# A recurrent graph layer: far targets scaled on ScalarE one node later, and five of them instead of four at places 1 to 3

## The chip, the cores and the metric

The kernel runs on one core of a Trainium2 chip (trn2). The core has a matrix engine, TensorE (PE in the profile, with its weight loads as PEld), and three engines for elementwise work: VectorE (DVE), ScalarE (ACT) and GpSimd (POOL). SyncE (SP) issues most of the DMAs. The metric is the time of one execution on the device in microseconds (us); lower is better.

## The reference, cut to what matters

The network has four layers over 64 graphs of 256 nodes with 256 features, and `adj` as each graph's weighted adjacency matrix. Layer 0 is a recurrence: node i sees a weighted sum of all other nodes' states, where the nodes before it have already been renewed.

```
d = sum(adj, -1);  dinv = 1/d (0 where d is 0)
norm_adjT = swapaxes(adj, 1, 2) * dinv[:, :, None]
for i in range(256):                       # a scan: one node after the other
    x     = h_e[:, i]
    x_par = einsum('bj,bjd->bd', norm_adjT[:, i], h)
    r, z  = sigmoid(x @ W_ioux.T + b_ioux + x_par @ W_iouh.T + b_iouh)
    hc    = tanh(x @ W_coux.T + b_coux + (x_par * r) @ W_couh.T + b_couh)
    h[:, i] = z * x_par + (1 - z) * hc
x = layernorm(x + h)
```

Layers 1 to 3 are a graph convolution and two attention layers, each with a residual and a layer norm. The change does not touch them.

## The kernel before, in words

**Tiling.** In the recurrence one tile of 128 x 128 holds a whole node: 64 graphs times two halves of the 256 features on the partitions, 128 features along the free side. The loop `for now in range(N)` is unrolled at build time and runs over the 256 nodes n; inside a `manual_schedule` the order of instructions on each engine is the order of the program text. U = 8 nodes make a block, and p = n % 8 is called the node's place here.

**Who adds what to whom.** `ACC` holds, for each node still to come, the weighted sum of the states it depends on; `sums[a]` is the tile of block a. A finished state j has to be added to all its later targets. They are shared out by distance:

- The next target, j + 1, gets it through the chain itself (`xp` from `zcc`, line 866).
- Targets up to the end of the next block are the list `to`, first target n + 1 where j = n - 1. The far end of the list, `FAR[p]` targets, goes to GpSimd; the rest, `near`, goes to VectorE as one *push* each: line 630, a multiplication by the weight and an addition to ACC in one instruction, which reads the state from PSUM (`keep`).
- At places 0 and 1 `behind` gives GpSimd eight more targets of the state that closed a block, in two groups of four.
- Everything older comes out of matrix products: `late` (from a ring `Hw` of states in SBUF, which DMAs fill from `hs`) and `early` (from states that were written to HBM, `Hd`). PE does such pieces as *fills* between the chain's own matmuls, ACT copies them out of PSUM (`copy_later`, line 256), DMAs carry them to and fro, and GpSimd adds them to ACC (lines 818 and 876).

**GpSimd's part.** `push_far` multiplies the state `hs` by the weights of all its far targets into the tile `far` (line 663, one instruction for all) and adds this to ACC (line 667). `far` has one buffer. Ahead of it, in each node, GpSimd makes `ready` (line 805), the next node's sum times dinv.

**The chain of a node.** PE transposes xp, ACT copies it to `xpT` (line 614); `next_of(copies, n)` may put one copy after it. PE makes the gate r (`rc`, `h_part`, line 605), ACT its sigmoid `rs` (line 824), PE transposes it, VectorE multiplies it with xpT (`rT`, line 828). Then VectorE makes `zx` and `v` (lines 846 and 853), PE the candidate, ACT its tanh (line 861), VectorE `zcc` (line 863) and the next xp (line 866). Pushes stand in two places on VectorE: `push(1)` and `push(5)` ahead of rT, and `push(3)` between v and zcc. What is left of a state's pushes comes in the next node. `x_part` (line 597) makes the part of the gates that depends on x alone, for the next node, on PE, after tanh's input.

Of the kernel before, what the change touches and what calls it, by code (L numbers as in the profile page):

```python
# [9 lines left out]
F32 = mybir.dt.float32  # L10
BF16 = mybir.dt.bfloat16
AF = mybir.ActivationFunctionType
# [7 lines left out]
P = 128  # L20
# [50 lines left out]
def _recurrence(tc, ident, Hd, x, adj, W_ioux, b_ioux, W_iouh, b_iouh, W_coux, b_coux, W_couh, b_couh, wide, then):  # L71
# [19 lines left out]
    nc = tc.nc  # L91
# [7 lines left out]
    XB = 4  # L99
    NG = B // 4  # L100
    HB = B // 2
    FAR = (2, 4, 4, 4, 4, 4, 3, 4)

    with ExitStack() as ctx:
        const = ctx.enter_context(tc.tile_pool(name="r_const", bufs=1))
# [42 lines left out]
        tmp = stage.enter_context(tc.tile_pool(name="r_setup", bufs=1))  # L148
# [41 lines left out]
        for w in range(2):  # L190
            first = (w * T - W + T // 2) % W
# [50 lines left out]
        copies = []  # L242
# [3 lines left out]
        def next_of(queue, n):  # L246
            if queue:
                queue.pop(0)(n)
# [344 lines left out]
        def x_part(G, n, kc, gates):  # L593
            a, u = divmod(n, U)
            h, i = divmod(u, U // 2)
            for o in range(2):
                nc.tensor.matmul(  # L597
                    G[o * B:(o + 1) * B], xqT[a, i // 2][:, i % 2, kc, h * B:(h + 1) * B],
                    WxT[:, kc, o, gates], start=False, stop=False, skip_group_check=True,
                )  # L600
# [9 lines left out]
        def flip(src, tag, n):  # L610
            pt = ps.tile([P, P], F32, tag="flip", name=f"{tag}_ps_{n}")
            nc.tensor.transpose(pt, src, ident)
            t = new(tag, n, 1)
            nc.scalar.copy(t, pt)  # L614
            return t

        def new(tag, n, bufs=2):
            return work.tile([P, P], F32, tag=tag, name=f"{tag}_{n}", bufs=bufs)

        def cell(j, m, count=1):  # L620

            a, u = divmod(m, U)
            k, i = divmod(m, T)
            return sums[a][:, u:u + count, :], tables[k]["S"][:, LAG + j - k * T, i:i + count]

        def push(count):
            for _ in range(min(count, len(pushes))):
                m, j = pushes.pop(0)
                acc, s = cell(j, m)
                nc.vector.scalar_tensor_tensor(  # L630
                    acc[:, 0, :], keep[:, j % 2, :], s, acc[:, 0, :], ALU.mult, ALU.add
                )
# [10 lines left out]
        def state(n):  # L643

            h = keep[:, n % 2, :]
            nc.vector.tensor_add(h, zcc, keep[:, 2, :])
            hs = new("hs", n, 7)
            nc.vector.tensor_add(hs, zcc, keep[:, 2, :])
            ring_in.append((n, hs))
            return hs  # L650

        def into_ring():
            n, hs = ring_in.pop(0)
            for o in range(2):
                to = Hw[n % W::W] if n < N - U else Hd[n]
                nc.sync.dma_start(to[..., o * P:(o + 1) * P], hs[o * B:(o + 1) * B])

        def push_far(j, hs, first, count):

            acc, s = cell(j, first, count)  # L660
            tmp = work.tile([P, 4, P], F32, tag="far", name=f"far_{j}_{first}", bufs=1)
            shape = [P, count, P]
            nc.gpsimd.tensor_mul(  # L663
                tmp[:, 0:count, :], hs.unsqueeze(1).to_broadcast(shape),
                s.unsqueeze(2).to_broadcast(shape),
            )
            nc.gpsimd.tensor_add(acc, acc, tmp[:, 0:count, :])  # L667

        tables = {k: {} for k in range(NB)}
        sums = {}  # L670
# [41 lines left out]
        work = ctx.enter_context(tc.tile_pool(name="r_work", bufs=2))  # L712
# [16 lines left out]
                x_part(G, 0, kc, gates)  # L729

        keep = ps.tile([P, 4, P], F32, tag="keep", name="keep")
        xp = new("xp", 0)
        nc.vector.tensor_scalar(xp, sums[0][:, 0, :], dinv[:, 0:1], None, ALU.mult)

        zcc = hs = None
        late_side = background = None
        behind = []
        x_left = x_side()
# [18 lines left out]
        for now in range(N):  # L757
            n = now
            k, i = divmod(n, T)
            p = n % U  # L760
            last = n + 1 == N

            xpT = flip(xp, "xpT", n)
            next_of(copies, n)

            far = []
            if n:

                assert all(j == n - 2 for _, j in pushes)
                hs = state(n - 1)  # L770
                end = min((n - 1) // U * U + 2 * U, N)
                to = list(range(n + 1, end))
                near = to[:len(to) - min(FAR[p], len(to) - 1)] if to else []
                far = to[len(near):]
                pushes += [(m, n - 1) for m in near]
                pushes.sort()
                if p == 0:

                    behind = [(n - 1, hs, m, 4) for m in range(end, min(end + U, N), 4)]

                if p > 3 or n >= N - U:
                    for _ in range(min(2, len(ring_in))):
                        into_ring()
# [23 lines left out]
                    dinv[:, n + 1:n + 2].to_broadcast([P, P]),  # L807
                )
            push(5)
            if far:  # L810
                push_far(n - 1, hs, far[0], len(far))
            if behind:
                push_far(*behind.pop(0))
            if p in (3, 4):
                half = slice((p - 3) * U // 2, (p - 2) * U // 2)
                for first, part in early_parts:
                    acc = sums[first // U][:, half]
# [32 lines left out]
            if not last:  # L850
                Sd = tables[kk]["Sd"][:, ii:ii + 1]
                v = keep[:, 3, :]
                nc.vector.scalar_tensor_tensor(v, zx, Sd, ready, ALU.mult, ALU.add)
                push(3)
                for kc in range(2):
                    x_part(rc, n + 1, kc, slice(0, 2))
                z = ps.tile([P, P], F32, tag="z", name=f"z_ps_{n + 1}")
                nc.scalar.copy(z, bias_z)
                for kc in range(2):
                    x_part(z, n + 1, kc, 2)  # L860
            nc.scalar.activation(c, c, AF.Tanh)
            zcc = new("zcc", n, 1)
            nc.vector.tensor_mul(zcc, zc, c)
            if not last:
                xp = new("xp", n + 1)
                nc.vector.scalar_tensor_tensor(xp, zcc, Sd, v, ALU.mult, ALU.add)
            for _ in range(2):
                next_of(copies, n)
# [554 lines left out]
def kernel(ctx: ExitStack, tc: tile.TileContext, ins, out):  # L1423
# [14 lines left out]
    def load_layers(load):  # L1438
        weights.extend(
            _load_layers(nc, wide, load, ins["L1_gnn_W"], ins["L1_gnn_b"], l2, l3)  # L1440
        )

    _recurrence(
        tc, ident, Hd, x, adj,
        *(ins["L0_gnn_" + n] for n in (
# [44 lines left out]
```

## Time and profile before

| | |
|---|---|
| median of 3 runs | 3351.88 us (3350.82 to 3364.95) |
| the profiled execution, its own time | 3353.51 us |
| its span, first to last instruction | 3351.7 us |
| VectorE busy | 2554.5 us (76%) |
| ScalarE busy | 1838.6 us (55%) |
| GpSimd busy | 1845.0 us (55%) |
| TensorE busy | 3131.6 us (93%) |
| pushes, line 630 | 1712, mean 343 ns |
| far multiplications, line 663 | 313, mean 973 ns |
| far additions, line 667 | 313, mean 1189 ns |

The profile follows one execution instruction by instruction. Busy time is the time in which an engine has at least one instruction of its own at work, and matmuls are pipelined, so that a busy PE need not be at its peak. A row of a group gives the engine, the operation, the tiles (out<-in), how often it stands, its busy time, the mean length of one, and the idle time of the engine just before. The waits view says which instruction waited for which, and for how long in total. In a timeline the square bracket shows how long the engine had been idle before an instruction and what released it.

The loop over the nodes fills the stretch from 139 to 1475 us; layers 1 to 3 come after it.

### The profile page before, as it was taken

Reading aid. Unit: us, or ns where it says so; the run is one execution under the profiler, and the core shown is the slowest. Engines: PE = TensorE matmul, PEld = TensorE weight load, DVE = VectorE, ACT = ScalarE, POOL = GpSimd, SP = SyncE. Lnnn points to the kernel's source line nnn. Section 1 sums busy time; section 2 is a strip of 40 time slices with the busy share of each in tenths; the row PEclk is TensorE's granted clock in tenths of the full one; section 3 lists DMA queues with packets and bytes.
Section 4 is the critical chain, followed back from the end, with each engine's and each line's share of the span. In section 5 each row is a group of like instructions: output and inputs, shape, how many; then the busy total and the mean of one; then the engine's idle time right before and its main releaser. Section 6 shows DMA issues by size and latency. Waiting matters only on the chain.

```text
span 3351.7 us, 78940 instructions
## 1 busy us (share of the span) xinstructions
PE 3131.6 (93%) x28584; PEld 2311.5 (69%) x28584; DVE 2554.5 (76%) x7381; ACT 1838.6 (55%) x4754; POOL 1845.0 (55%) x2165
## 2 busy tenths in 40 slices
PE   5799998998879998969999999999999999999997
PEld 4566665555545555547888888888888888888885
DVE  3487777776667878856888888888888888888885
ACT  0155554544445544535666666666666666666664
POOL 2377777766667878833444444444444444444443
PEclk7899999999999999989999999999999999999999
DMA  9856685788877675241221211122222222222210
GB/s 292 247 161 156 168 194 152 179 198 207 204 181 178 163 174 152 65 105 47 56 57 54 57 56 54 54 55 58 57 58 58 58 57 58 57 58 58 58 33 20
DMA packets 528608, 364.62 MB, mean 109 GB/s; under 512 B 246620, under 2 KB 494568, under 8 KB 522984
## 3 DMA queue, kind: packets, MB, share of 16 engines
q1 hardware_dynamic: 510520, 342.63, 39.6%
q10 hardware_dynamic: 17696, 16.91, 1.5%
q8 instruction: 229, 3.75, 0.5%
q14 instruction: 163, 1.34, 0.1%
HBM read 240.78 MB, written 99.61 MB: 102 GB/s over the span
## 4 chain that ended last, share of the span: by engine, by line
PE 77%; DMA 8%; DVE 7%; issue 2%; SPq 2%; ACT 2%; POOL 1%; DVEq 0%; ACTq 0%; POOLq 0%
PE mm L997 14%; PE rc L605 6%; PE rc L597 4%; PE s L1195 4%; PE mm_2f L997 3%; PE mm_3v L997 3%; PE mm_3f L997 3%; PE mm_2v L997 3%; PE late L521 3%; PE mm_t L997 3%; PE mm_2s L997 3%; PE mm_g L997 3%; PE mm_2w L997 3%; PE o L1230 3%; DVE ACC L630 3%; PE o L1221 3%
## 5 line engine op out<-in xcount | busy, mean ns | idle before, releaser
L1207 POOL TENSOR_TENSOR p3s<-p 128x256 f32<-128x256 f32 x512 | 358.9, 733 | 364.7 <-ACT p L1205 364.6
L630 DVE SCALAR_TENSOR_TENSOR ACC<-keep,S,ACC 128x128 f32<-128x128 f32 x1712 | 479.1, 343 | 16.9 <-POOL ACC L876 11.2
L997 PE MATMUL mm<-xT,weights 128*128 128x256 f32 x2048 | 483.7, 384 | 2.7 <-ACT xT L1094 2.7
L997 PEld LDWEIGHTS mm<-xT,weights 128*128 128x128 f32 x2048 | 386.0, 191 | 79.9 <-issue 25.5
L1204 DVE TENSOR_TENSOR p<-s,neg 128x512 f32<-128x512 f32 x512 | 317.6, 682 | 118.2 <-PE s L1195 118.2
L667 POOL TENSOR_TENSOR ACC<-ACC,far 128x384 f32<-128x384 f32 (+1 forms) x313 | 372.1, 1189 | 24.5
L663 POOL TENSOR_TENSOR far<-hs,S 128x384 f32<-128x384 f32 (+1 forms) x313 | 304.7, 973 | 4.7
L1205 ACT ACTIVATE p<-p 128x512 f32<-128x512 f32 x512 | 292.4, 626 | 1.6 <-DVE p L1204 1.6
L961 ACT ACTIVATE y<-y,shift,rstd 128x256 f32<-128x256 f32 x512 | 272.9, 599 | 26.6 <-DVE shift L959 22.7
L597 PE MATMUL rc<-WxT,xqT 128*64 128x256 f32 x2048 | 274.8, 390 | 1.1 <-issue 1.1
L1119 ACT ACTIVATE qk<-mm,weights 128x256 f32<-128x256 f32 x256 | 107.5, 471 | 301.9 <-PE mm L997 301.9
L805 POOL TENSOR_TENSOR ready<-ACC,dinv 128x128 f32<-128x128 f32 x255 | 102.1, 400 | 304.7 <-DVE ACC L630 304.2
L1108 POOL TENSOR_TENSOR y<-y,g 128x512 f32<-128x512 f32 x64 | 81.0, 1266 | 301.8 <-issue 301.8
L1244 DVE RECIPROCAL rT<-o 128x256 f32<-128x256 f32 x128 | 223.7, 1748 | 0.3 <-PE o L1221 0.2
L949 DVE BATCH_NORM_STATS2 st<-y 128x6 f32<-128x256 f32 x512 | 209.6, 409 | 13.1 <-POOL y L1108 10.3
L521 PE MATMUL late<-Hw,An 64*32 64x256 f32 x3840 | 166.7, 400 | 42.1 <-DMA Hw<-hs 18.8
L605 PE MATMUL rc<-WhT,rT 128*64 128x128 f32 x2048 | 172.5, 290 | 35.6 <-DVE rT L828 33.2
L824 ACT ACTIVATE rs<-rc 128x128 f32<-128x128 f32 x256 | 71.1, 278 | 245.0 <-PE rc L605 245.0
L605 PEld LDWEIGHTS rc<-WhT,rT 128*64 128x64 f32 x2048 | 109.1, 138 | 133.2 <-DVE rT L828 110.8
L953 POOL TENSOR_TENSOR rstd<-rstd,mhalf 128x2 f32<-128x2 f32 x256 | 173.8, 697 | 47.9 <-DVE rstd L952 34.6
L1066 POOL TENSOR_TENSOR dis<-dis,mhalf 128x2 f32<-128x2 f32 x64 | 44.9, 702 | 273.2 <-DVE dis L1065 261.8
L605 PE MATMUL rc<-WhT,xpT 128*64 128x128 f32 x2048 | 169.4, 286 | 18.1 <-ACT xpT L614 18.1
(162 smaller groups left out, 7255.4 us busy)
## 6 DMA issues: line engine op xcount, KB each, us to landing
xX<-in_x_dram ACTq DMA_DIRECT2D x16, 1024.0 KB
Us<-xu SPq DMA_DIRECT2D x64, 256.0 KB
xq<-in_x_dram SPq DMA_DIRECT2D x64, 256.0 KB
ACC<-Us SPq DMA_DIRECT2D x32, 512.0 KB
Es<-eu SPq DMA_DIRECT2D x64, 256.0 KB
early_sb<-Es SPq DMA_DIRECT2D x32, 512.0 KB
xin<-in_x_dram SPq DMA_DIRECT2D x64, 256.0 KB
ad<-in_adj_dram SPq DMA_DIRECT2D x64, 256.0 KB
```

The lines of the kernel that those rows point to most:

```text
L521: nc.tensor.matmul(pb[g][q * T:(q + 1) * T, e, :], An[rows, b].rearrange("p u s -> p (u s)"), Hw[rows, b, :], start=True, stop=True,)
L597: nc.tensor.matmul(G[o * B:(o + 1) * B], xqT[a, i // 2][:, i % 2, kc, h * B:(h + 1) * B], WxT[:, kc, o, gates], start=False, stop=False, s ...
L605: nc.tensor.matmul(G[o * B:(o + 1) * B], hT[:, kc * B:(kc + 1) * B], WhT[:, kc, o, g], start=False, stop=(kc == 1), skip_group_check=True,)
L630: nc.vector.scalar_tensor_tensor(acc[:, 0, :], keep[:, j % 2, :], s, acc[:, 0, :], ALU.mult, ALU.add)
L663: nc.gpsimd.tensor_mul(tmp[:, 0:count, :], hs.unsqueeze(1).to_broadcast(shape), s.unsqueeze(2).to_broadcast(shape),)
L667: nc.gpsimd.tensor_add(acc, acc, tmp[:, 0:count, :])
L961: nc.scalar.activation(y[:, c, :], y[:, c, :], AF.Identity, bias=shift[:, c:c + 1], scale=rstd[:, c:c + 1],)
L997: nc.tensor.matmul(pm[:, c, :], lhsT[:, k, c * P:(c + 1) * P], rhs[:, k, :], start=(k == 0), stop=(k == 1),)
L1204: nc.vector.tensor_add(p, s_ps[i], self.neg3)
L1205: nc.scalar.activation(p, p, AF.Exp, scale=ISQ)
L1207: nc.gpsimd.tensor_add(both, p[:, 0, :], p[:, 1, :])
L1244: nc.vector.reciprocal(rT, o_ps[:, 1, :])
```

## The change

`push_far` is split. `scale_far` reserves the far tile and lets ACT multiply the state by the weight of the first `begun` far targets, one activation (Copy, with the weight as its scale) for each; it returns a function that lets GpSimd multiply the targets that are left and add all of them to ACC. In the loop, `scale_far` is called right after the copy of xpT, for the far targets of the state that the node before had listed. GpSimd's part then comes at the old spot in this node, one node later than before. `begun` is 4, or 2 where copies are queued, and not more than there are targets. The groups of `behind` are still multiplied and added by GpSimd alone.

FAR rises by one at places 0 to 3, and the tile `far` from four to five targets. `push(3)` between v and zcc becomes `push(2)`. `xp` has one buffer instead of two.

```diff
-    FAR = (2, 4, 4, 4, 4, 4, 3, 4)
+    FAR = (3, 5, 5, 5, 4, 4, 3, 4)
...
         def push_far(j, hs, first, count):
+            scale_far(j, hs, first, count, 0)()
+
+        def scale_far(j, hs, first, count, begun):
             acc, s = cell(j, first, count)
-            tmp = work.tile([P, 4, P], F32, tag="far", name=f"far_{j}_{first}", bufs=1)
-            shape = [P, count, P]
-            nc.gpsimd.tensor_mul(
-                tmp[:, 0:count, :], hs.unsqueeze(1).to_broadcast(shape),
-                s.unsqueeze(2).to_broadcast(shape),
-            )
-            nc.gpsimd.tensor_add(acc, acc, tmp[:, 0:count, :])
+            tmp = work.tile([P, 5, P], F32, tag="far", name=f"far_{j}_{first}", bufs=1)
+            for e in range(begun):
+                nc.scalar.activation(tmp[:, e, :], hs, AF.Copy, scale=s[:, e:e + 1])
+
+            def finish():
+                if begun < count:
+                    shape = [P, count - begun, P]
+                    nc.gpsimd.tensor_mul(
+                        tmp[:, begun:count, :], hs.unsqueeze(1).to_broadcast(shape),
+                        s[:, begun:count].unsqueeze(2).to_broadcast(shape),
+                    )
+                nc.gpsimd.tensor_add(acc, acc, tmp[:, 0:count, :])
+
+            return finish
...
-        xp = new("xp", 0)
+        xp = new("xp", 0, 1)
...
-        zcc = hs = None
+        zcc = hs = far = None
...
             xpT = flip(xp, "xpT", n)
+            begun = 2 if copies else 4
             next_of(copies, n)
+            add_far = far and scale_far(*far, min(begun, far[-1]))
...
-                near = to[:len(to) - min(FAR[p], len(to) - 1)] if to else []
-                far = to[len(near):]
+                near = to[:len(to) - max(0, min(FAR[p], len(to) - 2))]
+                far = (n - 1, hs, to[len(near)], len(to) - len(near)) if near != to else []
...
-            if far:
-                push_far(n - 1, hs, far[0], len(far))
+            if add_far:
+                add_far()
...
-                push(3)
+                push(2)
...
-                xp = new("xp", n + 1)
+                xp = new("xp", n + 1, 1)
```

## The prediction

> **What bounds the kernel now.** I read the busy time of the stretch that layer 0's loop fills, then the waits inside it, then the timeline of single nodes. The windows view gives the loop (columns: busy us of PE, weight loads, DVE, ACT, POOL):
>
> ```profile
> 139.00:1475.00 1336.00, 1215.21 (x15980) 772.74 (x15978) 1014.43 (x3601) 660.55 (x2188) 961.73 (x1054) 0.98 0.66 166
> ```
>
> 256 nodes in 1336 us are 5.22 us a node. No engine is full, so the nodes hang on a chain. The waits view of the same stretch (us in total, times, longest) shows its links, and that GpSimd hardly holds anybody:
>
> ```profile
> ACT rs L824 <- PE rc L605: 245.0, 255, 4.7
> DVE zcc L863 <- ACT rc L861: 123.1, 135, 7.1
> DVE rT L828 <- PE rT_ps L826: 112.7, 175, 4.1
> PE late L521 <- DMA Hw<-hs: 18.8, 7, 5.6
> DVE ACC L630 <- POOL ACC L876: 11.2, 4, 5.0
> DVE keep L853 <- POOL ready L805: 9.9, 2, 6.1
> ```
>
> Each node runs xpT (ACT), rc (PE), rs (ACT), its transpose (PE), rT (DVE), rc again (PE), tanh (ACT, L861), zcc and xp (DVE), the next xpT. The timeline of a node at place 2 (start us, us) shows where pushes matter:
>
> ```profile
> 1132.98 0.27 ACT L614 COPY xpT<-xpT_ps 128x128 f32<-128x128 f32 x1 [0.36 <-PE xpT_ps L612]
> ...
> 1134.23 0.28 ACT L824 ACTIVATE rs<-rc 128x128 f32<-128x128 f32 x1 [0.98 <-PE rc L605]
> ...
> 1134.93 0.29 DVE L828 TENSOR_TENSOR rT<-rT_ps,xpT 128x128 f32<-128x128 f32 x1 [0.16 <-PE rT_ps L826]
> ...
> 1135.92 0.87 DVE L630 SCALAR_TENSOR_TENSOR ACC<-keep,S,ACC 128x128 f32<-128x128 f32 x3
> 1136.18 0.26 ACT L861 ACTIVATE rc<-rc 128x128 f32<-128x128 f32 x1 [0.45 <-PE rc L605]
> ...
> 1136.71 0.28 DVE L863 TENSOR_TENSOR zcc<-zc,rc 128x128 f32<-128x128 f32 x1
> ...
> 1137.79 0.27 ACT L614 COPY xpT<-xpT_ps 128x128 f32<-128x128 f32 x1 [0.36 <-PE xpT_ps L612]
> ```
>
> The reader is to see two things. Three pushes sit behind rT, and zcc starts straight after them (no idle time is shown), 0.53 us after tanh, where it starts 0.29 us after tanh at the places without them: VectorE is late there. And ACT is idle for 0.98 us just before rs, waiting for PE. The change spends that idle time.
>
> **What the Trainium skill says.** "ScalarE: Activation LUTs", section "What ACT_TABLE_LOAD costs": an ACTIVATE with immediate operands takes 186 ns + 0.833 ns an element, each pointer operand adds about 93 ns, and neighbours overlap by about 93 ns. The trace agrees: the layer norm's ACTIVATE (256 elements, two pointers) would be 186+213+186 = 585 ns, the trace has 598 as median, and four of them take
>
> ```profile
> 2005.86 2.08 ACT L961 ACTIVATE y<-y,shift,rstd 128x256 f32<-128x256 f32 x4
> ```
>
> so (2.08-0.60)/3 = 0.493 us from start to start. "Perfetto Trace Analysis", section "Tensor Engine Instruction": ACT, DVE and GpSimd are strict first in, first out. What stands behind a waiting or late scale on ACT therefore waits too; the rows of before do not show it at this spot. "SBUF — State Buffer", section "SBUF: two separate sides": GpSimd holds off a VectorE operation only if that is in a two-port mode or has two SBUF inputs. A push reads one operand from PSUM; its pitch is 0.26 us in nodes with and without GpSimd work. So a lighter GpSimd makes the pushes no faster: priced at nothing.
>
> **The change part by part.**
>
> *Pushes.* FAR goes from 29 to 33 targets in eight nodes. VectorE loses one push behind rT at places 1, 2 and 3, and one ahead of rT at place 0. The latter is worth nothing: VectorE idles 0.37 us ahead of rT there. Behind rT a push is 0.26 us, but tanh to next xpT cannot fall below 1.49 us: that is what places 4 to 7 take, where x_part and the transpose on PE set it. Places 1 and 2 take 1.61 (1136.18 to 1137.79), so 0.12 each is gained; place 3, whose last push depends on the one before it, takes 1.74, so 0.25. Over 30 blocks, the few nodes held elsewhere left out: 3.8 + 4.0 + 7.8, some **15.5 us gained**. PE is late next.
>
> *Scales on ACT.* In the built order 916 activations stand between xpT and rs: four at places 0 and 2 to 6, three at place 7, and at place 1 mostly one copy and two. No row has this operation. From L961: 0.493 less 128 elements (0.107) less one pointer (0.093) is 0.293 us a scale. From below, 0.265 if the pointer is hidden in part; from above, 0.386 if a second operand is fetched like a pointer. I take 0.293. Then rs can start 4 x 0.293 + 0.17 (the step between neighbouring activations such as zc and z) = 1.34 us after xpT; with three 1.05; at place 1 0.16 + 0.61 + 0.29 + 0.17 = 1.23. Today rs starts after 1.09 at place 0, 1.25 at places 1 to 3, and at places 4 to 7 after 1.08 (no fill on PE ahead of it), 1.22 (one fill) or 1.5 to 1.8. What stands queued behind the scales is rs, and behind rs the transpose, rT and the rest of the chain. Per place, over 31 blocks:
> - place 0: 0.25 x 31 = 7.6 us
> - place 1: nothing (1.23 below 1.25); place 7: nothing (1.05 below 1.08)
> - place 2: 0.09 x 29 = 2.7 us, and the wait below
> - place 3: 0.09 x 17 = 1.6 us; in 12 nodes VectorE reaches rT 0.22 later than the transpose and covers it
> - place 5: 1.0 us, place 6: 10 x 0.26 + 14 x 0.12, about 4.0 us
> - place 4: mostly under the push below.
>
> *Waits that are new.* The far buffer has one copy, so the first scale waits for the GpSimd add of the node before. This bites at place 2 only: at place 1 GpSimd starts its far add after the second scale (1.5 us after xpT), then adds three (1.00), scales four (1.04) and adds four (1.28) for the block behind, and with 0.08 between them ends 5.0 us after xpT. The next xpT comes at 4.81 - 0.12 = 4.69. I put the first scale, and so rs, 0.11 later in 24 nodes: 2.6 us. Second, at place 4 the push behind rT goes to the target that GpSimd adds as its fifth in that very node. Its add takes 1.28 + 0.28 = 1.55 us (rows of 2, 3 and 4 targets: 0.726, 1.002, 1.276) and ends about 3.2 to 3.4 us after xpT, while the push stands at 2.8 to 3.1 today. With the scales' own delay place 4 loses 4.4 us. Loss in all: 7.6+5.3+1.6+4.4+1.0+4.0 = **24 us**.
>
> *What covers the loss.* Place 0 lasts 5.44 us undisturbed, but 7.08 on average: in some blocks PE waits at the late fill (L521) for hs rows that DMAs bring to Hw. A delay of places 4 to 0 vanishes in such a wait as far as it reaches: taken block by block up to 7.6 us; I take 6, as some landings shift along. Without that cover it is paid in full.
>
> *Nothing.* The single xp buffer (its last reader is an earlier VectorE operation); the lighter GpSimd, as `ready` is waited for twice only; SP, which gets no DMA more or less. GpSimd loses nearly all far multiplications, at about 1 us each, beside the chain.
>
> Sum: -15.5 + 24 - 6 = +2.5, say **+3 us**. The profiled execution took 3353.51 (span 3351.7), 1.6 above the median of the runs, 3351.88; on the median's footing I predict 3355.
>
> **The rivals.**
> - *A draw* (0.62): as summed. All three prices cancel: between 0.28 and 0.32 us a scale the sum runs from -4 to +14 us.
> - *The scales fit* (faster): if rs is not late, only the push saving is left, -15.5 us, and -22 if PE gives way too (0.24 + 0.24 + 0.26 a block); only the second passes 0.5%. For it: 0.98 us of idle ACT. Against it: four scales at any price above 0.23 need more than 1.09 at place 0. About 3330 to 3336.
> - *ACT becomes the chain* (slower): a scale costs 0.386, where four stand in a row they hold rs until 4 x 0.386 + 0.17 = 1.71 us. Worked through the same list the loss is 92 us, less 15.5 and up to 18 of cover: +58, 3410. It passes 0.5% from about 0.33 us a scale. For it: no row of this form. Against it: L961 fits the page's pointer price.
> - *The change does nothing on ACT*: if the scales kept to GpSimd, only the later adds and pushes would remain; the built order excludes it.
>
> **How the numbers follow.** A measurement of this kernel can tell about 0.5% (17 us) from no change. Same 0.62. Slower 0.25: 0.12 for a scale over 0.33 us, the rest for no cover at place 0 together with more waits on GpSimd. Faster 0.13, for scales below 0.26 with more stalls absorbed. The range 3335 to 3382 takes in scale prices of about 0.26 to 0.335 and the disturbance by DMA waits (the runs shown spread over 14 us); the full second-operand case is left out.
>
> **What would show it.** In the profile after: activations of 128x128 to `far`, mean near 0.39 us and 0.29 from start to start; ACT busy up by some 290 us; GpSimd down by about 160; rs 1.34 us behind xpT at places 0 and 2; the wait of rs for PE nearly gone; tanh to xpT 1.49 at places 1 to 3; pushes 1592 instead of 1712. I am wrong if rs keeps its 1.1 us at place 0, if places 1 to 3 gain more than 0.25, or if a wait of ACT for GpSimd's add totals over 10 us.

## The result, and the profile after

The changed kernel takes 3354.73 us as median of 12 runs (3345.69 to 3363.22), the kernel before 3356.49 us beside it; the ratio is 0.9995 with a 95% interval of 0.9981 to 1.0009. No change can be told, as forecast. The execution in the profile took 3362.24 us, a long one of this kernel, so its total says little; its single nodes say a lot.

The windows view of the loop (columns as before):

```profile
136.00:1478.00 1342.00, 1213.24 (x15955) 773.55 (x15957) 978.13 (x3475) 901.31 (x3100) 805.80 (x915) 0.97 0.66 165
```

ACT rose from 661 to 901 us in the loop, GpSimd fell from 962 to 806, VectorE from 1014 to 978. The waits view of the loop:

```profile
DVE rT L841 <- PE rT_ps L839: 152.1, 205, 4.8
DVE zcc L876 <- ACT rc L874: 124.5, 134, 6.9
POOL ACC L676 <- ACT far L667: 96.3, 139, 2.9
PEld rT_ps L839 <- ACT rs L837: 87.2, 254, 0.6
ACT rs L837 <- PE rc L605: 17.4, 33, 3.1
PE late L521 <- DMA Hw<-hs: 16.3, 7, 3.8
DVE ACC L630 <- POOL ACC L676: 10.0, 31, 0.5
```

The wait of rs for PE, 245.0 us before, has gone to 17.4. That is no gain: rs now comes after the scales instead, PE's transpose waits longer for rs (62.7 to 87.2), and VectorE waits longer for the transpose ahead of rT (112.7 to 152.1). GpSimd's add now waits for ACT's scales (third line); that delays the chain only where VectorE or ACT in turn waits for the add. The last line is such a place: the push at place 4, 31 times, once a block. The timeline of a node at place 2, in the same block as the node shown of before:

```profile
1133.97 1.27 POOL L676 TENSOR_TENSOR ACC<-ACC,far 128x512 f32<-128x512 f32 x1
...
1134.98 0.27 ACT L614 COPY xpT<-xpT_ps 128x128 f32<-128x128 f32 x1 [0.24 <-PE xpT_ps L612]
...
1135.28 1.28 ACT L667 ACTIVATE far<-hs,S 128x128 f32<-128x128 f32 x4
...
1136.46 0.26 ACT L837 ACTIVATE rs<-rc 128x128 f32<-128x128 f32 x1
...
1138.13 0.61 DVE L630 SCALAR_TENSOR_TENSOR ACC<-keep,S,ACC 128x128 f32<-128x128 f32 x2
1138.38 0.26 ACT L874 ACTIVATE rc<-rc 128x128 f32<-128x128 f32 x1 [0.45 <-PE rc L605]
...
1138.68 0.29 DVE L876 TENSOR_TENSOR zcc<-zc,rc 128x128 f32<-128x128 f32 x1
...
1139.87 0.27 ACT L614 COPY xpT<-xpT_ps 128x128 f32<-128x128 f32 x1 [0.24 <-PE xpT_ps L612]
```

Both halves stand in it. Behind rT there are two pushes; zcc starts 0.30 us after tanh (1138.38 to 1138.68) and no longer 0.53, and tanh to the next xpT takes 1.49 us instead of 1.61. Ahead of it, rs starts 1.48 us after xpT instead of 1.25. The first scale starts as soon as GpSimd's add (1133.97 + 1.27 = 1135.24) has ended. The node takes 4.89 us instead of 4.81: what the pushes save here, the later rs takes back and a little more.

By place, medians of the xpT-to-xpT time in us, worked out from the starts of line 614 in the traces (at place 0 the undisturbed time, the lower quarter of the nodes):

| place | 0 | 1 | 2 | 3 | 4 | 5 | 6 | 7 |
|---|---|---|---|---|---|---|---|---|
| before | 5.44 | 4.81 | 4.81 | 5.02 | 4.76 | 5.22 | 4.63 | 4.63 |
| after | 5.67 | 4.69 | 4.90 | 4.79 | 4.80 | 5.22 | 4.73 | 4.63 |

### The profile page after: what moved, and what is told of

Its sections match the earlier page's. It is cut to its first block, busy times and chain, and to the rows that moved or that the text cites. A ratio compares the mean times of both kernels' runs of the same rounds, so it can differ in the third digit from the quotient of the medians.

```text
span 3360.5 us, 79856 instructions
## 1 busy us (share of the span) xinstructions
PE 3134.5 (93%) x28584; PEld 2315.3 (69%) x28584; DVE 2520.3 (75%) x7261; ACT 2080.4 (62%) x5670; POOL 1689.1 (50%) x2028
## 4 chain that ended last, share of the span: by engine, by line
PE 75%; DMA 7%; ACT 6%; DVE 4%; POOL 3%; issue 3%; SPq 2%; ACTq 0%; POOLq 0%; DVEq 0%
PE mm L1010 14%; PE rc L605 5%; PE rc L597 5%; PE s L1208 4%; PE mm_2f L1010 4%; PE mm_3v L1010 4%; PE mm_t L1010 3%; ACT far L667 3%; PE mm_3f L1010 3%; PE mm_2v L1010 3%; PE mm_g L1010 3%; PE mm_2s L1010 3%; PE mm_2w L1010 3%; PE o L1243 3%; PE tr_x L1000 3%
## 5 line engine op out<-in xcount | busy, mean ns | idle before, releaser
L676 POOL TENSOR_TENSOR ACC<-ACC,far 128x640 f32<-128x640 f32 (+2 forms) x312 | 404.6, 1297 | 143.8 <-ACT far L667 96.3
L630 DVE SCALAR_TENSOR_TENSOR ACC<-keep,S,ACC 128x128 f32<-128x128 f32 x1592 | 447.6, 343 | 24.3 <-POOL ACC L676 10.0
L667 ACT ACTIVATE far<-hs,S 128x128 f32<-128x128 f32 x916 | 295.3, 394 | 1.2
L962 DVE BATCH_NORM_STATS2 st<-y 128x6 f32<-128x256 f32 x512 | 209.6, 409 | 13.5 <-POOL y L1121 10.7
L521 PE MATMUL late<-Hw,An 64*32 64x256 f32 x3840 | 169.5, 407 | 39.5 <-DMA Hw<-hs 16.3
L841 DVE TENSOR_TENSOR rT<-rT_ps,xpT 128x128 f32<-128x128 f32 x256 | 74.2, 290 | 155.0 <-PE rT_ps L839 154.8
```

The source lines that it names most:

```text
L630: nc.vector.scalar_tensor_tensor(acc[:, 0, :], keep[:, j % 2, :], s, acc[:, 0, :], ALU.mult, ALU.add)
L667: nc.scalar.activation(tmp[:, e, :], hs, AF.Copy, scale=s[:, e:e + 1])
L962: nc.vector.bn_stats(st, y[:, c, :])
```

## The experiments

**One half each.** The first run keeps the saving of the pushes and gives all scales back to GpSimd, in the state's own node:

```diff
             next_of(copies, n)
-            add_far = far and scale_far(*far, min(begun, far[-1]))
...
-            if add_far:
-                add_far()
+            if far:
+                push_far(*far)
```

> The push half of the change alone: FAR, five targets and push(2) as in the changed kernel, but GpSimd scales every far target itself and in the state's own node, as before. Theory (two effects that cancel): the saving of the pushes behind rT stands alone, rs keeps 1.09 us behind xpT at place 0 and 1.25 at places 1 to 3, tanh to the next xpT is about 1.49 us at places 1 to 3, and the time is 10 to 16 us below before. Rival A (waits for DMAs set the pace, so neither half moves the time): within 4 us of before. Rival B (the relief of GpSimd is what pays for the scales): GpSimd is now fuller than before, so slower than before by 10 us or more.

Measured: 3347.07 us beside 3354.59 of before, ratio 0.9974 (0.9962 to 0.9987): 7.5 us faster by the medians, 9 by the ratio. Places 1 to 3 take 4.69, 4.69 and 4.72 us, rs keeps 1.09 and 1.25. Rival A and rival B are out: the half moves the time, and with a GpSimd that is fuller than before. The gain is smaller than the 10 to 16 us expected. In this trace places 1 to 3 took 13.5 us less over 30 blocks and place 0 took 9.7 more; but it is one trace of each kernel, and the runs of one kernel differ by 4 to 6 us (standard deviation). The first place to look is the late fills (L521), where PE waits for the DMAs that carry states to the ring. The number before the first arrow of such a row is PE's idle time ahead of the fills, in us. Before:

```profile
L521 PE MATMUL late<-Hw,An 64*32 64x256 f32 x3840 | 166.7, 400 | 42.1 <-DMA Hw<-hs 18.8 <-DMA Hs<-Hd 5.5 <-POOL ACC L667 5.2
```

and in this run:

```profile
L521 PE MATMUL late<-Hw,An 64*32 64x256 f32 x3840 | 169.1, 407 | 42.3 <-DMA Hw<-hs 22.5 <-DMA Hs<-Hd 7.2 <-DMA Es<-eu 5.8
```

More of it is put down to the ring's DMAs (18.8 to 22.5), but the whole is the same, 42.1 and 42.3. So these rows don't show where the rest of the saving went.

The second run has the scales, but FAR and the third push as before:

```diff
-    FAR = (3, 5, 5, 5, 4, 4, 3, 4)
+    FAR = (2, 4, 4, 4, 4, 4, 3, 4)
...
-                push(2)
+                push(3)
```

> The scale half alone: ACT scales up to four far targets one node later, but FAR and push(3) as before. Theory: rs 1.34 us behind xpT at places 0, 2, 3, 4 and 6, tanh to xpT stays 1.61 to 1.74 at places 1 to 3; by place 7.6 + 2.7 + 1.6 + 2.3 + 1.0 + 4.0 = 19 us lost, some 6 of it covered by DMA waits at place 0: 11 to 19 us above before. Rival A: within 4 us of before. Rival B: GpSimd loses its multiplications, so faster by 5 us or more.

Measured: 3362.90 us, ratio 1.0023 (1.0013 to 1.0034): 8 us slower. rs starts 1.34 us behind xpT at places 0, 2, 3, 4 and 6, as worked out. Rivals A and B are out; the loss is on the right side, but below the lower end of 11 us. The two halves, -0.26% and +0.23%, make up the change's -0.05%.

**How many scales.** The changed kernel with three scales at most:

```diff
-            begun = 2 if copies else 4
+            begun = 2 if copies else 3
```

> The changed kernel with at most three scales on ACT in a node instead of four; GpSimd multiplies one target more. Theory: three scales let rs start 1.05 us behind xpT, ahead of PE everywhere, so rs is no later than before at places 0, 3, 6 (1.09, 1.25, 1.08 to 1.22); left are the saving of the pushes, 15.5 us, and at place 4 the push that waits for GpSimd's add, 4 to 6 us: 8 to 13 us below before. Rival A: within 4 us of before. Rival B (the loss comes from the wait of ACT for GpSimd's add and from the delay by one node, not from how many scales there are): as the changed kernel.

Measured: 3355.03 us, ratio 0.9999 (0.9988 to 1.0011): a miss. By its total both rivals would do, for it is within 4 us of before and like the changed kernel; the trace and the next run speak against them. rs is on time (1.09 at place 0, 1.25 at places 1 to 3), and places 1 to 3 take 4.69 us each, so that part held. Place 4 did not: 5.01 us instead of 4.76, some 9 us over 30 blocks. The timeline of a place 4 in this run:

```profile
243.39 1.55 POOL L676 TENSOR_TENSOR ACC<-ACC,far 128x640 f32<-128x640 f32 x1
...
244.57 0.26 ACT L874 ACTIVATE rc<-rc 128x128 f32<-128x128 f32 x1 [0.31 <-PE rc L605]
...
244.97 0.35 DVE L630 SCALAR_TENSOR_TENSOR ACC<-keep,S,ACC 128x128 f32<-128x128 f32 x1 [0.55 <-POOL ACC L676]
245.24 0.28 DVE L876 TENSOR_TENSOR zcc<-zc,rc 128x128 f32<-128x128 f32 x1
```

The push, and zcc behind it on the same engine, wait 0.55 us for the far add, and zcc comes 0.67 us after tanh. The fourth scale's work had moved to GpSimd, ahead of this add. Another 9 us or so sit at places 5 to 7, in single long nodes of this one trace; place 0 did not grow in it. The fourth run takes both waits for GpSimd away:

```diff
-    FAR = (3, 5, 5, 5, 4, 4, 3, 4)
+    FAR = (3, 5, 5, 5, 5, 4, 3, 4)
...
-            begun = 2 if copies else 4
+            begun = 0 if p == 1 else 3
```

> As the run with three scales, and the two waits for GpSimd taken away: no scale on ACT at place 1, so that GpSimd ends its groups there before the next xpT, and FAR 5 at place 4 too, so that no push behind rT goes to a target that GpSimd adds to in the same node. Theory: nothing but the saving of the pushes is left: 12 to 17 us below before, rs as before at all places, no wait of a push for the far add. Rival A: within 4 us of before. Rival B: no better than the run with three scales, since those two waits cost nothing.

Measured: 3351.55 us, ratio 0.9985 (0.9975 to 0.9995): 3 us faster by the medians, 5 by the ratio; place 4 back at 4.75 us, places 1 to 3 at 4.69 to 4.76, rs on time everywhere. It beats the run with three scales by some 4 us (4.2 by the means of the runs, with a 95% uncertainty of 3, as in all that follows), so rival B falls, but it stays far from 12 to 17, and so near 4 that its total alone doesn't exclude rival A. Again place 0 grew, by 6.6 us over 30 blocks.

**The ring's DMAs left out.** Those runs left one question: is the price of a push too high, or does place 0 swallow the saving? In each of these kernels the DMAs into the ring can be left out. The late products then work on zeros, so their share of the result is missing, while their instructions stay:

```diff
             n, hs = ring_in.pop(0)
-            for o in range(2):
+            for o in range(2 if n >= N - U else 0):
```

> The kernel before without the DMAs that carry each state from hs into the ring Hw (only the last eight, which go to HBM, stay). The late products then work on zeros: their share of the result is left out, their instructions stay. It is the reference for the two runs beside it. Theory (place 0 waits in part of the blocks for these DMAs): place 0 falls from a mean of 7.1 us to below 6, 25 to 40 us below before. Rival (place 0 is long by other DMA traffic): less than 10 us below before.

> The push half alone, with the same DMAs left out (the late products work on zeros). Theory (a saving at places 1 to 3 is given back where place 0 then waits longer for the ring's DMAs): without these waits the saving of the pushes shows in nearly every block, 12 to 16 us below the run without the ring of the kernel before. Rival (the price of a push behind rT was simply set twice too high): 6 to 10 us below it, as with the ring.

> The changed kernel with the same DMAs left out (the late products work on zeros). Theory: no cover is left for the scales and none takes the pushes' saving away, so 24 less 15.5, some 6 to 12 us above the run without the ring of the kernel before. Rival (gain and loss cancel whatever the DMAs do): within 4 us of it.

Measured, in this order: 3279.96, 3271.11 and 3288.79 us (3354.79 for before on that chip; the ratios to before are 0.9777, 0.9749 and 0.9796, each within 0.0021). The first was expected 25 to 40 us below before and is 75 below: place 0 falls to 5.27 us in nearly all blocks, under the 5.44 that I had taken as undisturbed. The row of the late fills in it, 1.1 us of idle time in place of 42.1:

```profile
L521 PE MATMUL late<-Hw,An 64*32 64x256 f32 x3840 | 162.1, 388 | 1.1 <-issue 1.1
```

The changed kernel is 8.8 us above its reference by the medians, near the 8.5 that gain and loss sum to without cover; by the means it is 5.4 above, with an uncertainty of about as much, so the rival (within 4 us) is not excluded. Above the push half beside it the changed kernel stands by 17.7 us (16.3 by the means, uncertainty about 5). The push half is 8.9 below its reference, which is inside the rival's 6 to 10 and not the theory's 12 to 16. With five runs each that is not settled, so both were run again with the fourth kernel beside them:

> The kernel before without the DMAs into the ring, once more, as the reference on this chip. Every theory: 2.0 to 2.4% below before.

> The push half without the DMAs into the ring, once more, since the first comparison fell between two readings. Theory (the saving shows in nearly every block): 11 to 16 us below the run beside it of the kernel before without the ring. Rival (the price was set too high): 6 to 9 us below it.

> The kernel with three scales on ACT, none at place 1, and FAR 5 at place 4, without the DMAs into the ring (the late products work on zeros). Theory (nothing of the chain is lost in it, and what it missed with the ring went into waits for DMAs): as fast as the push half without the ring, within 4 us, so 0.24 to 0.45% below the kernel before without the ring beside it. Rival (scales on ACT cost something even where rs is on time): 5 us or more above the push half without the ring.

Measured: 3284.68, 3272.83 and 3269.94 us (ratios to before 0.9790, 0.9757 and 0.9751, each within 0.0020). The push half is 11.9 us below the run beside it; over both chips the medians of ten runs each are 3271.97 and 3283.73, so 11.8, from a spread of about 4 us a run. The means give 12.0 with an uncertainty of about 4: neither the 15.5 of the prediction nor the rival's 10 is clearly excluded. The kernel with three scales apart is 14.7 us below, level with the push half: where rs is on time, scales on ACT cost nothing that these runs can tell (0.1 us by the means, uncertainty about 5). This kernel is also the clearest case of a gain that the ring takes away: it is 3 to 5 us below before with the ring's DMAs, and 13 to 15 below its reference without them. Against the medians of all ten runs of the reference the changed kernel stands 5.1 us above, against the five beside it 8.8.

**The price of a scale, doubled.**

```diff
-            for e in range(begun):
+            for e in 2 * list(range(begun)):
```

> The changed kernel with every scale on ACT issued twice, so up to eight stand ahead of rs. Theory: rs comes 8 x 0.293 + 0.17 = 2.51 us behind xpT at places 0 and 3 to 6, 1.17 more than in the changed kernel, and at places 1 and 7 0.6 to 0.7 more; about 30 x (5 x 1.17 + 0.6 + 0.6), 190 us above the changed kernel, less what DMA waits cover, so 150 to 200 us above. Rival (ACT has room, other waits set the pace): less than 60 us above.

Measured: 3566.63 us in one run, 212 above before and so as much above the changed kernel: ACT has no room left. rs comes 2.51 us behind xpT at places 0 and 3 to 6, as computed. The total is 12 us above the upper end. The list in the expectation left out place 2, which takes 1.18 us more than in the changed kernel, and as it stands it sums to 212 and not to 190; that 212 was also measured is chance. By the medians of the nodes (at place 0 the lower quarter) a block takes 8.0 us more, 247 us over 31 blocks, an estimate; some 35 of these did not arrive. The trace shows where they were covered. PE's idle time ahead of the late fills is nearly gone, 5.6 us where the kernel before has 42.1 and the changed kernel 39.5:

```profile
L521 PE MATMUL late<-Hw,An 64*32 64x256 f32 x3840 | 162.2, 392 | 5.6 <-DMA Hs<-Hd 1.5 <-issue 0.8 <-DMA A<-in_adj_dram 0.3
```

Place 0 takes 7.08 us on average and 6.84 undisturbed; in the changed kernel these are 7.47 and 5.67. The tile's view of the scales (ns, minimum, median and maximum of one):

```profile
L667 ACT ACTIVATE far<-hs,S x1832: 384/389/416, 147.0 to 1676.0; 128x128 f32<-128x128 f32 x184
```

Of the kernels that leave nothing out the push half alone is the fastest, 0.9974 of before; the changed kernel stood at 0.9995 in its own comparison.

Side by side, in us against the kernel before (without the ring's DMAs, against the kernel before without them); less is faster. The first column is an estimate: the differences of the median nodes of a block, at place 0 of the lower quarter, times 31 blocks. The others are measured totals, by medians and by ratios or means:

| | from its undisturbed nodes | with the ring's DMAs | without them |
|---|---|---|---|
| push half | -15.5 to -16.6 | -7.5 to -9 | -12 |
| three scales apart | -15.5 | -3 to -5 | -13 to -15 |
| scale half | +14 | +8 | not run |
| the change | +3.5 to +5 | -2 | +5 to +9 |
| the change less the push half | +20 to +21 | +6 to +7 | +16 to +18 |

## Why the prediction was right, point by point

- **The bound.** The chain of a node sets the time, and the idle 0.98 us of ACT ahead of rs was the resource that the change spends. Doubling the scales showed it.
- **The price of a scale.** Put at 0.293 us; four take 1.28 us at place 2, (1.28 - 0.39)/3 = 0.297 from start to start. The mean of one is 394 ns, expected 0.39 us. rs: 1.34 expected and measured at place 0. Only the split was other: the first scale can start 0.16 us after xpT, and rs follows the last by 0.29. ACT's busy time rose by 242 us and not by 290: a scale lasts 394 ns, but its neighbours start 0.29 us apart and so overlap.
- **The pushes.** 1592 of them, as counted. Tanh to xpT is 1.49 us at places 1 to 3, PE's floor. The saving was put at 15.5 us. The medians of the nodes bear it out; the totals without the ring give 11.8, with an uncertainty of about 4.
- **The waits for GpSimd.** At place 2 the add of the node before ends after the next xpT and rs comes 0.14 us later than the scales alone would make it; 0.11 was expected. The push at place 4 waits in each block. ACT's idle time ahead of the scales is 1.2 us in all, far under the 10 that were named as a sign of being wrong, since most of that delay falls within the copy to xpT. In the changed kernel place 4 lost 4.9 us over 30 blocks (expected 4.4), in the run with three scales 9 (expected 4 to 6).
- **The loss.** Put at 24 us. Without the ring the change costs 16 to 18 us over the push half, with an uncertainty of about 5, so the loss was put too high. Of gain and loss together 8.5 should have been left; 5.1 to 8.8 were measured by the medians.
- **The cover: the step that was mis-sized.** The prediction let the DMA waits at place 0 hide 6 us of the loss and none of the gain. That a delay vanishes in these waits is shown by the doubled scales, where PE's idle time ahead of the late fills falls to 5.6 us, from 42.1 before and 39.5 in the changed kernel. But the waits work both ways. The clearest case of a lost gain is three scales apart, 13 to 15 us without the ring and 3 to 5 with it. The push half goes the same way; its totals alone (12 and 8) lie too near each other to tell, but only half of what its nodes save arrives with the ring. The loss shrinks too, and by more than 6: from 16 to 18 us over the push half to 6 or 7. So too large a loss and a cover that takes from the gain as well nearly cancel in the sum. That the total, +3 predicted and 2 below measured, came so close is partly luck. That no change can be told is not: each half was measured alone, and they have opposite signs and about the same size.
- **Small slips.** In the list of the loss, 10 x 0.26 + 14 x 0.12 is 4.3 and not about 4.0, and 0.25 x 31 is 7.75 and not 7.6. They change nothing.
- **What stays open.** How the ring takes a gain away. A block that is 0.5 us shorter up to place 3 would reach the ring's transfers sooner and wait longer there, and place 0 grew by 9.7 and 6.6 us in the traces of the push half and of three scales apart; but PE's idle time ahead of the late fills is the same with the push half, and place 0 did not grow in the trace with three scales at most. It is also open why three scales apart is 4 us behind the push half with the ring (4.2 by the means of their runs, uncertainty 3) and level with it without. Issuing the ring's DMAs earlier or from another queue wasn't tried.

## What to carry to other kernels

Idle time of an engine in the middle of a chain is room only up to its length: list it place by place, and add up start-to-start steps, not mean durations, before filling it. An operation handed to a half-idle engine costs nothing that could be told here while it ends before the chain's next instruction there, and once it does not, its excess, as far as no other wait covers that. Where a loop has waits for transfers at a fixed spot, they can shrink gains and losses alike, as here, so the effect of each half is best measured with and without them. And before a wait is blamed, add up all rows of the waiting instruction: one row can grow while the whole stays.

## What the runs showed of the hardware that I had not expected

Leaving out the ring's transfers, 496 DMAs of 32 KB, took 75 us off, more than the 50 us by which place 0 exceeded its lower quarter ((7.08 - 5.44) x 31). In the traces place 0 gives 55.6 us of the 72.6 over 30 blocks, and place 5 another 9.7. The granted clock in the loop was 0.98 before and 0.99 without the ring, too small a step for a loop that is 5% shorter.

Blocks that looked undisturbed gained as well: place 0 fell from 5.44 to 5.27 us in them. The traces show no wait for data there. PE's queue of weight loads has semaphore instructions for the late fills (L521; ns, minimum, median and maximum of one), before and without the ring:

```profile
L521 PEldq EVENT_SEMAPHORE  x203: 51/51/4764, 179.7 to 1416.6; - x102
L521 PEldq EVENT_SEMAPHORE  x83: 51/51/51, 192.0 to 1348.0; - x83
```

The longest of before, 4.76 us, is a wait for a transfer. But in the undisturbed blocks four of them stand ahead of the first fill, each 51 ns long, the shortest there is here, and the fill's first weight load starts 1.82 us after xpT. Without the ring none stands there, and it starts at 1.68. So the instructions that ask for transfers which have long landed go with 0.14 of the 0.17 us a block.

GpSimd's additions are linear in the number of targets: 0.726, 1.002 and 1.276 us for 2, 3 and 4, and 1.55 for 5, as extrapolated.
